# Two-layer gated cross-attention: order of the quads in layer 0, and later inputs loaded inside its loop

## Chip, cores and metric

The kernel runs on one core of a Trainium2 chip. The metric is the device time in microseconds of one execution. Engines are named as in the profile: PE (TensorE matmul), PEld (its weight loads), DVE (VectorE), ACT (ScalarE), POOL (GpSimd), SP (SyncE, which here only issues DMAs).

## The reference

```python
x = x + tanh(g_xattn[0]) * L0_xattn(layernorm(x), ctx, ...)   # 16 heads of 16, scores over 375 keys
x = x + tanh(g_ffn[0])   * L0_ffn(layernorm(x), ...)          # a gated recurrence over the 32 items
x = x + tanh(g_xattn[1]) * L1_xattn(layernorm(x), ctx, ...)   # 16 heads of 64
x = x + tanh(g_ffn[1])   * L1_ffn(layernorm(x), ...)          # 64 experts, 8 for each row, and a shared one
```

`x` is 32 items of 112 rows of 256, `ctx` 32 items of 375 rows of 128, all float32. The change concerns the first line alone: for each item, queries from the normalised `x`, keys and values from `ctx`, softmax over 375 keys for each of 16 heads, the weighted values, and an output projection.

## The kernel before, in words

The kernel has four stages, one after the other: layer 0's attention (in the profile from the start to about 702 us), its recurrence (to about 900 us), layer 1's attention with the routing, and the experts. Items come in eight groups of four (`G = 4`). The tiles `xs[g]` and `cts[g]` hold a group's `x` and its transposed context for the whole kernel.

Layer 0's attention works in *quads*: quad `n` is heads `4*(n%4)` to `4*(n%4)+3` of item `n // 4`, four heads of 16 channels, each on its own 32 partitions (rows 0 to 15 of the 32 hold the channels, row 16 a one in the keys and, in the second round, the negated maximum in the queries). One quad needs:

- the keys: `keys0(n)` makes the keys of two quads, `n` and `n + 1`, with one product `pk` (L414); ACT adds the bias (`k`, L419), and eight DMAs on SP's queue copy 16 rows each into `kT` (L421). There are six `kT` tiles.
- the queries of a whole group: `queries0` (product `pq` L396, DVE `q` L401, sixteen DMAs `qp` on SP's queue, L405). They need the group's statistics (`rstd0`: DVE L142 and L143, then POOL `rs` L371 and L372) and the turned normalised rows (`turned0`: DVE `xn` L379, PE L386).
- the scores twice. `quad(n, js, m, ks)` makes scores `sc` of quad `n` for two heads (L447), of which DVE takes the negated maximum `nm` (L451); and, for quad `m = n - 2`, whose maxima are known, transposed scores `st` with the maximum already subtracted (L462), of which ACT takes the exponential `pT` (L468). `with_max(n)` turns the maxima (`pm`, L474) and adds them to the queries (`qa`, DVE L478).
- `values0(b, kc)`: a third of an item's values (`pv`, L432; ACT copy L436), and `values_of(n)`: the weighted values `pav` (L491), copied by DVE (`oU`, L495).
- for each item, once: `divided` (`pn`, L502), `turned_back` (`pb`, L514), `output_rows` (`po`, L179), with DVE's `to_a` L183, `x` L172 and new statistics.

The order on PE, DVE and ACT is written out by hand (`manual_schedule`): each of these engines runs its instructions in the order of the program. SP and POOL are ordered by the tile framework. `sc` and `st` share a ring of five PSUM buffers (`ps_s`), everything else on PE a ring of three (`ps_m`). One iteration `n` of the loop (L530) is, before the change:

```python
quad(n, (0, 1), n - 2, (2, 3))
values_of(n - 3); keys0(n + 2) if n is even; values0(b, g) if g < 3; with_max(n - 1)
quad(n, (2, 3), n - 2, (0, 1))
# then, by n: rstd0 / turned0 / queries0 of the next group, divided / turned_back / output_rows
```

Before the loop, SP loads the first group's `x` and `ctx`, and POOL issues the loads of the other seven groups (L327, L330). Behind these fourteen loads in POOL's queue stand its memsets of `qp`, `v` and `nm` (L344 to L357), the first group's `rs` (L371, L372), and the halving of a weight of a later stage (`sdn`, L664).

Of the kernel before, what the change touches and what calls it, by code (L numbers as in the profile page):

```python
# [39 lines left out]
B, S, D = 32, 112, 256  # L40
# [3 lines left out]
G = 4  # L44
NG = B // G
# [20 lines left out]
def flamingo_kernel(ctx: ExitStack, tc: tile.TileContext, a: dict, out: bass.AP):  # L66
    nc = tc.nc
# [59 lines left out]
    xs = [const.tile([S, G, D], F32, tag=f"x{g}", name=f"x{g}") for g in range(NG)]  # L127
# [181 lines left out]
    with ExitStack() as att:  # L309
        cpool = att.enter_context(tc.tile_pool(name="ctxT", bufs=1))  # L310
        cts = [cpool.tile([DC, G, LKV], F32, tag=f"c{g}", name=f"c{g}") for g in range(NG)]


        with ExitStack() as ph:
# [8 lines left out]
            nc.sync.dma_start(cts[0], a["ctxT"][:, 0:G, :])  # L323
            nc.sync.dma_start(wv, a["wv0"])
            nc.sync.dma_start(wo, a["wo0"].rearrange("(c p) m -> p c m", p=128))
            for g in range(1, NG):
                nc.gpsimd.dma_start(  # L327
                    xs[g], a["x"][g * G : (g + 1) * G].rearrange("b s d -> s b d")
                )
                nc.gpsimd.dma_start(cts[g], a["ctxT"][:, g * G : (g + 1) * G, :])  # L330


            one = wp.tile([128, 1], F32, tag="one", name="one0")
# [28 lines left out]
            ps_s = ph.enter_context(tc.tile_pool(name="ps_s0", bufs=5, space=PSUM))  # L362
            ps_m = ph.enter_context(tc.tile_pool(name="ps_m0", bufs=3, space=PSUM))
            xTs, qas, pTs, outs = {}, {}, {}, {}

            def rstd0(g):
                t0 = g * G
                for b in range(t0, t0 + G):
                    row_stats(b)
                rs = small.tile([S, G], F32, tag="rs", name=f"rs0_{g}")  # L370
                nc.gpsimd.tensor_scalar(rs, stats[:, t0 : t0 + G, 1], EPS, None, ALU.add)  # L371
                nc.gpsimd.tensor_tensor(rs, rs, half, ALU.pow)  # L372
                return rs

            def turned0(g, rs):
                xT = xTs[g] = kvp.tile([128, 2, GT], F32, tag="xT", name=f"xTa_{g}", bufs=1)
                xn = work.tile([S, G, D], F32, tag="xn", name=f"xn_a0_{g}")
                for j in range(G):
                    nc.vector.tensor_scalar(  # L379
                        xn[:, j, :], xs[g][:, j, :], stats[:, g * G + j, 0:1], rs[:, j : j + 1],  # L380
                        ALU.subtract, ALU.mult,
                    )
                for c in range(2):
                    pt = ps_m.tile([128, GT], F32, tag="mm", name=f"ptx_a0_{g}_{c}")
                    for j in range(G):
                        nc.tensor.transpose(  # L386
                            pt[:, j * S : (j + 1) * S], xn[:, j, c * 128 : (c + 1) * 128],
                            ident[:S, :S],
                        )
                    nc.vector.tensor_copy(xT[:, c, :], pt)  # L390
# [19 lines left out]
            def keys0(n):  # L410

                b, i = n // 4, n % 4 // 2
                pk = ps_m.tile([128, LKV], F32, tag="mm", name=f"pk0_{n}")
                nc.tensor.matmul(  # L414
                    pk, wk[:, 128 * i : 128 * i + 128], cts[b // G][:, b % G, :],
                    start=True, stop=True,
                )
                k = kvp.tile([128, LKV], F32, tag="k", name=f"k0_{n}")
                nc.scalar.activation(k, pk, AF.Identity, bias=cols[:, C_BK + i : C_BK + i + 1])  # L419
                for h in range(8):  # L420
                    nc.sync.dma_start(  # L421
                        kTs[(n + h // 4) % 6][h % 4 * 32 : h % 4 * 32 + 16, :],
                        k[16 * h : 16 * h + 16, :],
                    )
# [4 lines left out]
            def values0(b, kc):  # L429
                pv = ps_m.tile([KC, 2, NH // 2, 16], F32, tag="mm", name=f"pv0_{b}_{kc}")  # L430
                for r in range(2):
                    nc.tensor.matmul(  # L432
                        pv[:, r], cts[b // G][:, b % G, kc * KC : (kc + 1) * KC],
                        wv_of[:, r, r], start=True, stop=True,
                    )
                nc.scalar.copy(  # L436
                    vs[b % 2][:, kc, :, :16].rearrange("p (a r) j -> p r a j", r=2), pv
                )

            def quad(n, js, m, ks):  # L440


                if 0 <= n < 4 * B:
                    b, g, j0 = n // 4, n % 4, n // 4 % G * S
                    for j in js:
                        sc = ps_s.tile([S, LKV], F32, tag="s", name=f"sc0_{n}_{j}")
                        nc.tensor.matmul(  # L447
                            sc, qps[b // G % 2][32 * j : 32 * j + 32, g, j0 : j0 + S],
                            kTs[n % 6][32 * j : 32 * j + 32, :], start=True, stop=True,
                        )  # L450
                        nc.vector.tensor_reduce(  # L451
                            nms[n % 3][:, j, 16:17], sc, AX.X, ALU.max, negate=True
                        )
                if 0 <= m < 4 * B:
                    if m not in pTs:
                        pTs[m] = pp.tile([KC, 4, NKC, S], F32, tag="pT", name=f"pT0_{m}")
                    st = {
                        j: ps_s.tile([KC, NKC, S], F32, tag="s", name=f"st0_{m}_{j}") for j in ks
                    }
                    for kc in range(NKC):  # L460
                        for j in ks:
                            nc.tensor.matmul(  # L462
                                st[j][:, kc, :],
                                kTs[m % 6][32 * j : 32 * j + 32, kc * KC : (kc + 1) * KC],
                                qas[m][32 * j : 32 * j + 32, :], start=True, stop=True,
                            )
                    for j in ks:
                        nc.scalar.activation(pTs[m][:, j], st[j], AF.Exp)  # L468

            def with_max(n):  # L470

                b, g, j0 = n // 4, n % 4, n // 4 % G * S
                pm = ps_m.tile([128, S], F32, tag="mm", name=f"pm0_{n}")
                nc.tensor.transpose(  # L474
                    pm, nms[n % 3].rearrange("p h j -> p (h j)"), ident[:S, :S]
                )
                qa = qas[n] = kvp.tile([128, S], F32, tag="qa", name=f"qa_{n}", bufs=3)
                nc.vector.tensor_tensor(  # L478
                    qa, pm, qps[b // G % 2][:, g, j0 : j0 + S], ALU.add
                )  # L480

            def values_of(n):
                b, g = n // 4, n % 4
                pT, v = pTs.pop(n), vs[b % 2]
                del qas[n]
                if g == 0:
                    outs[b] = kvp.tile([128, 4, S], F32, tag="oU", name=f"oU_{b}")
                po = ps_m.tile([128, S], F32, tag="mm", name=f"pav0_{n}")
                for kc in range(NKC):
                    for j in range(4):  # L490
                        nc.tensor.matmul(  # L491
                            po[32 * j : 32 * j + 32, :], v[:, kc, 4 * g + j, :], pT[:, j, kc, :],
                            start=(kc == 0), stop=(kc == NKC - 1),
                        )
                nc.vector.tensor_copy(outs[b][:, g, :], po)  # L495
# [33 lines left out]
            rs = None  # L529
            for n in range(4 * B + 6):  # L530
                b, g = n // 4, n % 4
                quad(n, (0, 1), n - 2, (2, 3))
                if 0 <= n - 3 < 4 * B:
                    values_of(n - 3)
                if n % 2 == 0 and n + 2 < 4 * B:
                    keys0(n + 2)
                if b < B and g < NKC:
                    values0(b, g)
                if 0 <= n - 1 < 4 * B:
                    with_max(n - 1)  # L540
                quad(n, (2, 3), n - 2, (0, 1))
                if b // G + 1 < NG and b % G == 1 and g == 3:
                    rs = rstd0(b // G + 1)
                if b // G + 1 < NG and b % G == 2 and g == 1:
                    turned0(b // G + 1, rs)
                if b // G + 1 < NG and b % G == 2 and g >= 2:
                    queries0(b // G + 1, g - 2)
                if g == 3 and b >= 1:
                    divided(b - 1)
                elif g == 0 and b >= 2:  # L550
                    turned_back(b - 2)
                elif g == 1 and b >= 2:
                    output_rows(pools, "a0", b - 2, outs.pop(b - 2), wo, 2, R_BO0, 0)
# [510 lines left out]
    for b in range(B):  # L1064
# [9 lines left out]
        if b % G == G - 1:  # L1074
            g = b // G
# [58 lines left out]
```

## Time and profile before

| | us |
|---|---|
| three runs | 2758.73, 2759.26, 2775.71 |
| median | 2759.26 |
| the profiled execution | 2965.47, span 2963.8 |
| PE busy in it | 2466.7 (83%) |
| DVE, ACT, POOL busy | 1787.5, 1158.1, 589.3 |

A profile gives each instruction with its engine, source line, start and duration, and what ended the idle time before it. `x2` behind a line counts the instructions merged into it. In the chain of waits a line is start, length and what ran; in the timeline it is start, length, engine, line, operation, tiles and shapes, and in square brackets the engine's idle time before it and its releaser. In the table of stretches the columns are the stretch and its length, the busy time of PE, PEld, DVE, ACT and POOL with counts, the clock granted to PE as a share of full speed, the DMA engines' busy share, and GB/s. `SPq` is a DMA being issued on SP's queue.

### The profile page before, as it was taken

To read this page: it belongs to the slowest core of one execution; us is meant where nothing else is said; L and a number is where in the kernel's file an instruction comes from. 1 tells how busy PE (TensorE), PEld (TensorE's weight loads), DVE (VectorE), ACT (ScalarE), POOL (GpSimd) and SP (SyncE) were. 2 spreads that over 40 slices of the span, in tenths; PEclk is the share of its full clock that TensorE was granted. 3 is DMA by queue.
4 is the path that set the end of the run, shared out by engine and by line. 5 is a ranking of instruction groups with operands and counts; after the bars stand their busy time and mean duration, and the time that the engine had idled before them with its cause. 6 is when DMAs were issued, how large, how long until landed. Compare 5 with 4: busy or idle time off the path is not lost.

```text
span 2963.8 us, 57837 instructions
## 1 busy us (share of the span) xinstructions
PE 2466.7 (83%) x20884; PEld 1900.2 (64%) x20884; DVE 1787.5 (60%) x4995; ACT 1158.1 (39%) x3019; POOL 589.3 (20%) x671
## 2 busy tenths in 40 slices
PE   4999999999997999897979999897976478888820
PEld 2666676777995776675757666575754366776720
DVE  2666666665327667575666767566665445555557
ACT  1433444443333554443535444443533133333310
POOL 3000000000000001204031211304032465555520
PEclk9999999999999999998989999998988699999965
DMA  5111100114001000101010000101011955555469
GB/s 170 28 26 26 26 24 24 27 29 159 2 1 43 1 1 20 36 1 55 1 43 13 30 27 11 45 1 55 1 37 54 306 172 151 148 146 151 130 183 271
DMA packets 121528, 198.21 MB, mean 67 GB/s; under 512 B 27399, under 2 KB 97113, under 8 KB 117664
## 3 DMA queue, kind: packets, MB, share of 16 engines
q1 hardware_dynamic: 78624, 102.50, 12.6%
q0 software_dynamic: 30176, 79.57, 8.2%
q10 hardware_dynamic: 12448, 12.45, 1.3%
q8 instruction: 171, 2.80, 0.4%
q14 instruction: 109, 0.89, 0.1%
HBM read 104.11 MB, written 82.71 MB: 63 GB/s over the span
## 4 chain that ended last, share of the span: by engine, by line
PE 66%; DVE 12%; issue 7%; DMA 5%; POOL 3%; SPq 3%; another core or an unknown queue 2%; ACT 1%; POOLq 0%; DVEq 0%; ACTq 0%
PE pv L710 6%; PE sc L447 5%; PE pk L695 5%; PE pt_a L761 5%; PE ps_a L732 5%; PE pav L782 4%; PE st L462 4%; PE pq L682 4%; PE po_a L797 3%; PE pg L590 3%; PE pav L491 3%; PE pg L611 3%; DMA y<-yrows 2%; PE py L1021 2%
## 5 line engine op out<-in xcount | busy, mean ns | idle before, releaser
L737 ACT ACTIVATE p_a<-ps_a,nmax_a 112x375 f32<-112x375 f32 x512 | 286.8, 572 | 430.8 <-DVE nmax_a L736 407.5
L1032 POOL DMA_INDIRECT yrows<-yblk,dst x288 | 280.9, 975 | 221.2 <-ACT yblk L1025 80.7
L468 ACT ACTIVATE pT<-st 125x336 f32<-125x336 f32 x512 | 202.7, 448 | 310.4 <-PE st L462 310.4
L710 PE MATMUL pv<-wv,c 128*125 128x256 f32 x768 | 227.1, 407 | 107.5 <-DVE oT L787 104.8
L451 DVE TENSOR_REDUCE nm<-sc 112x1 f32<-112x375 f32 x512 | 256.3, 541 | 90.5 <-PE st L462 64.2
L761 PEld LDWEIGHTS pt_a<-ident,p_a 112*125 112x125 f32 x1536 | 236.5, 196 | 104.3 <-issue 22.7
L301 POOL DMA_INDIRECT xrows<-row,at x256 | 247.9, 968 | 248.3 <-DVE at L299 171.6
L447 PE MATMUL sc<-kT,qp 32*112 32x375 f32 x1024 | 268.3, 532 | 17.7 <-DMA kT<-k 14.0
L736 DVE TENSOR_REDUCE nmax_a<-ps_a 112x1 f32<-112x375 f32 x512 | 245.2, 540 | 35.3 <-PE ps_a L732 26.9
L761 PE MATMUL pt_a<-ident,p_a 112*125 112x112 f32 x1536 | 240.2, 279 | 18.7 <-issue 16.0
L462 PE MATMUL st<-qa,kT 32*125 32x112 f32 x3072 | 238.5, 287 | 0.0
L695 PE MATMUL pk<-c,wk 128*128 128x375 f32 x512 | 218.1, 509 | 3.9 <-issue 3.6
L710 PEld LDWEIGHTS pv<-wv,c 128*125 128x125 f32 x768 | 130.9, 197 | 127.6 <-DVE oT L787 114.4
L462 PEld LDWEIGHTS st<-qa,kT 32*125 32x125 f32 x3072 | 192.3, 187 | 15.9 <-DVE nm L451 15.2
L732 PE MATMUL ps_a<-kT,qT 64*112 64x375 f32 x1024 | 198.6, 507 | 0.0
L782 PEld LDWEIGHTS pav<-pT_a,v 125*64 125x64 f32 x3072 | 148.0, 137 | 69.7 <-issue 51.4
L749 DVE TENSOR_SCALAR p_a<-p_a,inv_a 112x375 f32<-112x375 f32 x512 | 178.8, 412 | 4.6
L699 ACT COPY kT<-pk 128x375 f32<-128x375 f32 x256 | 121.3, 474 | 149.3 <-PE pk L695 80.0
L782 PE MATMUL pav<-pT_a,v 125*64 125x112 f32 x3072 | 176.5, 263 | 0.3 <-issue 0.2
L996 PE MATMUL ph<-wall,xbT 128*128 x896 | 147.1, 294 | 20.1 <-issue 13.2
L195 POOL TENSOR_SCALAR rs<-stats 112x4 f32<-112x4 f32 (+1 forms) x9 | 2.0, 226 | 735.3 <-DVE stats L143 735.2
L797 PE MATMUL po_a<-wo,oT 128*112 128x256 f32 x512 | 144.3, 402 | 3.4 <-issue 3.3
(227 smaller groups left out, 4390.8 us busy)
## 6 DMA issues: line engine op xcount, KB each, us to landing
xblk<-xrows SPq DMA_DIRECT2D x288, 140.0 KB
y<-yrows SPq DMA_DIRECT2D x32, 896.0 KB
kT<-k SPq DMA_DIRECT2D x512, 23.4 KB
xrows<-blank POOLq DMA_DIRECT2D x1, 8960.0 KB
wall<-in_w_up SPq DMA_DIRECT2D x8, 1024.0 KB
wall<-in_w_down ACTq DMA_DIRECT2D x8, 1024.0 KB
c<-in_ctxT POOLq DMA_DIRECT2D x7, 750.0 KB
yrows<-yblk,dst POOLq DMA_INDIRECT x288
```

The lines of the kernel that those rows point to most:

```text
L301: disjoint("xrows", nc.gpsimd.indirect_dma_start(out=xrows[:, :], out_offset=bass.IndirectOffsetOnAxis(ap=at[:, j, k : k + 1], axis=0), in ...
L447: nc.tensor.matmul(sc, qps[b // G % 2][32 * j : 32 * j + 32, g, j0 : j0 + S], kTs[n % 6][32 * j : 32 * j + 32, :], start=True, stop=True,)
L451: nc.vector.tensor_reduce(nms[n % 3][:, j, 16:17], sc, AX.X, ALU.max, negate=True)
L462: nc.tensor.matmul(st[j][:, kc, :], kTs[m % 6][32 * j : 32 * j + 32, kc * KC : (kc + 1) * KC], qas[m][32 * j : 32 * j + 32, :], start=True ...
L695: nc.tensor.matmul(pk, wk[:, c * 128 : (c + 1) * 128], cts[b // G][:, b % G, :], start=True, stop=True,)
L710: nc.tensor.matmul(pv[:, i, :], ct[:, (lo + i) * KC : (lo + i + 1) * KC], wv[:, g * 256 : (g + 1) * 256], start=True, stop=True,)
L732: nc.tensor.matmul(sc, qT[r0 : r0 + 64, 2 * g + i, j0 : j0 + S], kT[r0 : r0 + 64, i, :], start=True, stop=True,)
L736: nc.vector.tensor_reduce(nmax[:, j : j + 1], sc, AX.X, ALU.max, negate=True)
L737: nc.scalar.activation(p[:, j, :], sc, AF.Exp, bias=nmax[:, j : j + 1], accum_out=tot[:, j : j + 1],)
L761: nc.tensor.transpose(pt[:, j * S : (j + 1) * S], p[:, j, kc * KC : (kc + 1) * KC], ident[:S, :S],)
L782: nc.tensor.matmul(po[64 * r : 64 * r + 64, i, :], v[:, kc, 64 * j : 64 * j + 64], pT[:, kc, j * S : (j + 1) * S], start=(kc == 0), stop=( ...
L1032: disjoint("yrows", nc.gpsimd.indirect_dma_start(out=yrows[:, :], out_offset=bass.IndirectOffsetOnAxis(ap=dst32[:, 2 * n + i : 2 * n + i + ...
```

## The change

The loads of groups 1 to 7 leave POOL's queue. They are issued on ACT's queue inside the loop, a pair at the first quad of each group for the group that follows. Inside an iteration, `values_of` and `with_max` stand between the two calls of `quad`, and `keys0` and `values0` stand behind the second. Line numbers grow by up to 3.

```diff
-            for g in range(1, NG):
-                nc.gpsimd.dma_start(
-                    xs[g], a["x"][g * G : (g + 1) * G].rearrange("b s d -> s b d")
-                )
-                nc.gpsimd.dma_start(cts[g], a["ctxT"][:, g * G : (g + 1) * G, :])
...
+            def inputs(g):
+                nc.scalar.dma_start(
+                    xs[g], a["x"][g * G : (g + 1) * G].rearrange("b s d -> s b d")
+                )
+                nc.scalar.dma_start(cts[g], a["ctxT"][:, g * G : (g + 1) * G, :])
...
                 b, g = n // 4, n % 4
+                if b // G + 1 < NG and b % G == 0 and g == 0:
+                    inputs(b // G + 1)
                 quad(n, (0, 1), n - 2, (2, 3))
                 if 0 <= n - 3 < 4 * B:
                     values_of(n - 3)
+                if 0 <= n - 1 < 4 * B:
+                    with_max(n - 1)
+                quad(n, (2, 3), n - 2, (0, 1))
                 if n % 2 == 0 and n + 2 < 4 * B:
                     keys0(n + 2)
                 if b < B and g < NKC:
                     values0(b, g)
-                if 0 <= n - 1 < 4 * B:
-                    with_max(n - 1)
-                quad(n, (2, 3), n - 2, (0, 1))
```

## The prediction

> **What bounds the kernel now.** I read the chain of waits first, over the opening 60 us. It shows what the start hangs on.
>
> ```profile
> 7.32 17.75 DMA c<-in_ctxT
> 25.08 0.28 issue
> 25.36 0.55 POOL c L330
> 25.91 3.13 POOL qp L344 x2
> 29.04 2.64 POOL v L350 x2
> ...
> 32.71 0.86 POOL sdn L664
> 33.57 1.03 POOL rs L372
> 34.62 0.43 DVE xn_a L379
> ```
>
> POOL issues fourteen loads; the later ones wait for earlier ones to land. Behind them in its queue stand its memsets and the inverse deviation `rs`, and the first normalised rows wait for `rs`. The statistics were ready at 11.01 (last L143, timeline), so the core idles until 34.62.
>
> Second, the timeline of one ordinary item, for what a quad costs. An iteration has two halves (`quad`): two score products (sc, L447) beside six transposed ones (st, L462). F is the first, S the second.
>
> ```profile
> 316.27 0.57 PE L447 MATMUL sc<-kT,qp 32*112 32x375 f32 x2
> ...
> 317.12 0.41 PE L514 MATMUL pb<-ident,on 112*128 112x112 f32 x2
> 317.18 1.00 DVE L451 TENSOR_REDUCE nm<-sc 112x1 f32<-112x375 f32 x2 [0.53 <-PE st L462]
> 317.34 0.79 ACT L468 ACTIVATE pT<-st 125x336 f32<-125x336 f32 x2 [0.66 <-PE st L462]
> 317.46 0.59 PEld L447 LDWEIGHTS sc<-kT,qp 32*112 32x112 f32 x4
> ...
> 318.24 0.73 PEld L462 LDWEIGHTS st<-qa,kT 32*125 32x125 f32 x12 [0.19 <-DVE nm L451]
> ...
> 319.08 0.54 PEld L491 LDWEIGHTS pav<-pT,v 125*32 125x32 f32 x24
> ```
>
> S starts at 316.27 and lasts 0.85 (pb follows at 317.12). DVE reads its maxima until 318.18, and only then, 1.97 after S began, does st of the next F find a free buffer (`ps_s` has five; st2 takes that of sc3). F so lasts 1.62 in place of 0.85. A half needs 1.97 - 0.85 = 1.12 us of other PE work behind it, or PE waits. PE looks 83% busy on the page because its ends are modelled; this wait is inside.
>
> Third, the timeline once per group of four items, where the queries are copied.
>
> ```profile
> 264.39 4.94 SPq L421 DMA_DIRECT2D kT<-k  x8
> ...
> 269.43 12.18 SPq L405 DMA_DIRECT2D qp<-q  x16
> ...
> 281.71 8.20 SPq L421 DMA_DIRECT2D kT<-k  x9
> ...
> 283.63 1.64 PE L447 MATMUL sc<-kT,qp 32*112 32x375 f32 x2 [2.76 <-DMA kT<-k]
> ```
>
> SP issues 24 copies back to back; the next keys, ready at 274.8, leave at 281.71, and PE waits 2.76. The stretch table then shows the granted clock halved.
>
> ```profile
> 283.50:287.00 3.50, 3.37 (x40) 2.77 (x40) 1.10 (x2) 0.79 (x2) 0.00 (x0) 0.50 0.16 41
> ```
>
> [...] Here waits of 1.48 to 2.76 were followed by a 0.5 clock in four of seven groups, waits of 1.08 to 1.53 not in three: it depends on the phase.
>
> **The change, part by part.**
>
> *Loads off POOL.* Removed: 21.8 us between POOL's `sdn` load (ends 4.07) and its memsets (25.91). The memsets, 6.4 us, then end at 10.5; the statistics end at 11.0; rs 0.25, sdn 0.86 and rs 1.03 with small gaps give 13.3. xn starts there and not at 34.62: -21.3. The first group's inputs and weights remain, about 2.8 MB, at the 285 GB/s of the first 40 us some 10 us: in place before 15. If x0 lands sooner without the other 8 MB, up to 1.2 more.
>
> *Loads on ACT.* Fourteen issues of about 0.45 (the two weight loads on ACT took 0.40 and 0.45), 6.3 us in all, in ACT's 310 us of waiting for st (waits view): nothing on the path; without that cover 6.3. In the built order every DMA waits for the last one on its completion semaphore, eight in rotation: a load waits for key copies an iteration old (landed), with the exponentials queued behind it on ACT; the seventh and eighth key copies, and in the first group one query copy, wait on SP for a load. A pair is 1.2 MB, 4.2 us at 285 GB/s. In the loop those rows are needed an iteration later: nothing, at most 1 us a group. In the first group the query copy may lose up to 1 us; I take 0.5. Start: -20.8, bounds -17 (all 4.2 us exposed) and -22.5.
>
> *The order inside an iteration.* No instruction is added. From the timeline, PE work in the gaps: pav 0.71, pk 0.73, pv 0.55, pm 0.25, pb 0.34, pn 0.57, po 1.05. Before, F to S held pav, pk, pv, pm (enough), S to F only pb, po, nothing or pn, for quads 0 to 3. Waits by the 1.12 rule: 0.78, 0.07, 1.12, 0.55; the trace has 0.77, 0.06, 1.11, 0.53. Sum 2.5 of an item's 17.91.
> After, F to S holds pav and pm, 0.96: 0.16 short. S to F holds pk and pv (1.28), pv and po (1.60), or for quad 3 pn alone: 0.39 (0.55 less the 0.16 S lost). Quad 2 pays more: behind po DVE runs to_a, x and two statistics, so its maxima of F end 2.7 us after F begins (304.51 to 307.13, and 0.06); S is reached after 1.81: 0.87. Quad 0's S finds its buffers free. Sum 0.16 + 0.87 + 0.16 + 0.39 = 1.6. Gain 0.9 an item.
>
> *Once per group.* Quads 0 to 7 gain 1.65, 14 and 15 0.9. Around quad 8 DVE's four statistics (2.2 us, 246.52 to 248.73) make S wait 1.8 in place of 2.0 spread before; at quad 9 pv hides 0.53 of PE's 1.46 wait for xn: together 0.4. Against: quad 10's k now comes after S (S waits for DVE as above, half ends F + 3.5), pk and two exponentials: its copies leave at F + 5.1, before at F + 3.1 to 3.9. SP then needs the same 19.2 (264.39 to 283.63) to quad 14, so this stretch loses 1.2 to 2.0, say 1.6, whatever PE saves in it; PE waits about 4 us there, and the halved clock, which cost 2 to 3.5 us in four of seven groups, comes nearly always: -1.3; the shorter xn wait returns 0.4. Net +0.45; seven groups 3.2. Outside them: quads 110 on, 4.5 items, 4.0; quads 3 to 9 of the start 1.2. Total -8.4, bounds +8 (clock lost in other places too) and -25 (no clock loss, SP's copies faster without a profile).
>
> *Key copies elsewhere.* k leaves SP about 1.3 later in its iteration. A copy lands 1.8 to 1.9 after issue (chain of waits); by my timing the second row lands at F + 6.9 for a use at F + 8.5: nothing.
>
> Sum: -20.8 - 8.4 = -29.2 of the profiled execution's 2965.47 us (span 2963.8). The runs' median is 2759.26, 206 less; where the profile adds these the trace doesn't say, so I carry the microseconds over unscaled: 2730.
>
> **Rivals.** (A) SP's queue decides more than one stretch: order gains nothing and loses about 1.2 us a group, 8 in all: 2759 - 21 + 8 = 2746. For: SP's 24 copies; against: SP idles outside that stretch. (B) The order pays fully: DVE's tails fit better than my hand timing, half of 2.5 us for 28 items and no clock loss: 35 us with the start 56: 2703. For: PE waits in three of four gaps; against: DVE's chain of 1.97 per half stays. (C) Slower: key rows late. Each of some 55 key products outside the queue stretch now has 1.6 us of slack; if landing takes over 3.5 us (now 1.9), every second quad waits. At 0.4 us each the start's gain is gone; at 1.05 it is 58: 2759 - 21 + 58 = 2796. [...] DMA engines are 10% busy. (D) The loads stay early or x0 and c0 become the wait: the built order has the loads among the activations, and 10 us of transfer end before 15; at worst 10 back: 2740, inside the forecast's range.
>
> **How the numbers follow.** Forecast 0.68, with D, own range 2715 to 2743; A 0.13; B 0.13; C 0.06. About 1% (27.6 us) can be told from no change. The forecast's middle lies just past it, so 0.42 of its 0.68 is faster, with B 0.55; its other 0.26 and A make 0.39 within; C 0.06 slower. The range takes in A and part of B: 2712 to 2749.
>
> **What would show it.** Right: xn near 13 us; first S waits of 0.16 and no wait in quads 1 and 3's F; 0.9 quad 2 S waits; the key wait per group grown to about 4 us, then a 0.5 clock. Wrong: key waits on ordinary even quads, xn later than 17, an ordinary item above 17.9 us.

## The result, and the profile after

The changed kernel takes 2750.94 us (median of 20 runs, 2746.51 to 2764.03) where the kernel before takes 2761.38 (20 runs, 2754.49 to 2777.43): a ratio of 0.9959, 95% interval 0.9944 to 0.9974, which is 10.4 us. In a later set of runs the same pair gave 2972.07 and 2981.45 us (e7 below): 0.9958, 0.9935 to 0.9980. The prediction said 29.2, and its range of 2712 to 2749 us ends just below the measured time. One run each of e7, e11, e14 and e16 below counts as slow (over 1.5% above the fastest of its kernel); without it no median moves by more than 0.9 us.

The chain of waits of the changed kernel has no pieces in the first 60 us, so the timeline stands in for it. Columns: start, length, engine, line, operation, tiles, and in brackets the idle time before and what ended it.

```profile
3.48 0.60 POOL L135 DMA_DIRECT2D sdn<-in_ws_down  x1
4.07 3.14 POOL L339 MEMSET qp<- 128x1792 f32 x2
...
11.33 0.59 POOL L372 TENSOR_SCALAR rs<-stats 112x4 f32<-112x4 f32 x1 [0.89 <-DVE stats L143]
...
12.01 2.16 POOL L667 TENSOR_SCALAR sdn<-sdn 128x256 f32<-128x256 f32 x1
12.05 1.40 DVE L335 COPY kT<-one 128x375 f32<-128x375 f32 x5
14.14 1.05 POOL L373 TENSOR_TENSOR rs<-rs,half 112x4 f32<-112x4 f32 x1
15.22 1.39 DVE L380 TENSOR_SCALAR xn_a<-x,stats,rs 112x256 f32<-112x256 f32 x4 [1.77 <-POOL rs L373]
...
19.18 0.35 ACTq L362 DMA_DIRECT2D x<-in_x  x1
...
28.30 2.12 PE L448 MATMUL sc<-kT,qp 32*112 32x375 f32 x5 [5.39 <-DMA qp<-q]
```

POOL goes straight from its loads to its memsets; the 21.8 us of loads are gone. The first normalised rows start at 15.22 and not at 34.62, the first score product at 28.30 and not at 46.26.

The timeline of an ordinary item, quads 1 and 2 of it:

```profile
297.61 0.57 PE L448 MATMUL sc<-kT,qp 32*112 32x375 f32 x2
297.62 0.58 PE L463 MATMUL st<-qa,kT 32*125 32x112 f32 x6
...
299.42 0.57 PE L448 MATMUL sc<-kT,qp 32*112 32x375 f32 x2
299.58 0.47 PE L463 MATMUL st<-qa,kT 32*125 32x112 f32 x4
...
303.73 1.29 PE L448 MATMUL sc<-kT,qp 32*112 32x375 f32 x4
304.59 0.73 PEld L463 LDWEIGHTS st<-qa,kT 32*125 32x125 f32 x12 [0.19 <-DVE nm L452]
304.59 0.91 PE L463 MATMUL st<-qa,kT 32*125 32x112 f32 x12
305.43 0.90 PE L415 MATMUL pk<-c,wk 128*128 128x375 f32 x2
```

F of quad 1 (297.61) has st at once; S of quad 1 (299.42) has it 0.16 later; S of quad 2 (303.73) has it 0.86 later. The first pn of one item to the first pn of the next is 292.54 to 309.51, or 16.97; before it was 17.91.

The once-a-group stretch, the same group as was shown of the kernel before, and the granted clock behind it (columns of the stretch table as before; the clock is the column with 0.54):

```profile
246.79 5.26 SPq L422 DMA_DIRECT2D kT<-k  x8
252.16 10.87 SPq L406 DMA_DIRECT2D qp<-q  x16
263.13 11.98 SPq L422 DMA_DIRECT2D kT<-k  x13
265.09 1.15 PE L448 MATMUL sc<-kT,qp 32*112 32x375 f32 x3 [3.46 <-DMA kT<-k]
```

```profile
266.00:269.50 3.50, 3.50 (x53) 2.77 (x49) 1.62 (x4) 0.79 (x2) 0.00 (x0) 0.54 0.13 34
```

PE now waits 3.46 us for key rows where it waited 2.76. Over the seven groups these waits are 2.83, 3.30, 3.46, 3.61, 2.80, 2.74 and 4.13, or 3.27 in the mean; before the mean was 1.84.

One warning on the two profiles. They do not come from like conditions. Between the first query product of layer 1 and its last output product (the tile views, before first, then after) lie 1349 us before and 1246 after:

```profile
L682 PE MATMUL pq<-xTb,wq x512: 352/352/743, 938.8 to 2178.8; 128*128 128x224 f32 x171
L797 PE MATMUL po_a<-wo,oT x512: 376/379/470, 973.4 to 2287.6; 128*112 128x256 f32 x171
```

```profile
L685 PE MATMUL pq<-xTb,wq x512: 352/352/739, 914.2 to 2063.4; 128*128 128x224 f32 x171
L800 PE MATMUL po_a<-wo,oT x512: 379/379/470, 949.4 to 2160.5; 128*112 128x256 f32 x171
```

In the five later sets of runs, on chips 2, 10, 7, 8 and 8 by the record, the kernel before took 2963 to 2983 us; its profiled execution of 2965.47 is of that kind. The record names no chip for the runs of the result. The same changed kernel took 1365 us for this stretch in e7's profile (920.0 to 2285.4), so the 103 us are not the change's doing. I take the 206 us between profile and median for two chips, not for a cost of profiling; that it is the chip was not tested. They lie behind layer 0. In layer 0 the profiles of the changed kernel are nearer to each other: the last item's first `pn` stands at 674.01 in the profile after and at 680.75 in e7's. The kernel before, cut behind layer 0, took 713.0 us on chip 2 and 708.8 on chip 8; the changed one 696.2 and 697.9. I read differences of under 5 us between chips as undecided.

### The profile page after: what moved, and what is told of

Its sections match the earlier page's. It is cut to its first block, busy times and chain, and to the rows that moved or that the text cites. A ratio compares the mean times of both kernels' runs of the same rounds, so it can differ in the third digit from the quotient of the medians.

```text
span 2745.6 us, 57911 instructions
## 1 busy us (share of the span) xinstructions
PE 2411.1 (88%) x20884; PEld 1882.0 (69%) x20884; DVE 1776.0 (65%) x4995; ACT 1164.1 (42%) x3019; POOL 581.4 (21%) x657
## 5 line engine op out<-in xcount | busy, mean ns | idle before, releaser
L448 PE MATMUL sc<-kT,qp 32*112 32x375 f32 x1024 | 264.1, 542 | 33.3 <-DMA kT<-k 24.2
L713 PE MATMUL pv<-wv,c 128*125 128x256 f32 x768 | 217.9, 393 | 49.1 <-DVE oT L790 47.4
L771 DVE COPY pT_a<-pt_a 125x448 f32<-125x448 f32 x128 | 78.8, 616 | 115.7 <-PE pt_a L764 115.6
L448 PEld LDWEIGHTS sc<-kT,qp 32*112 32x112 f32 x1024 | 87.2, 178 | 90.6 <-issue 45.5
```

The costliest lines, as they stand in the source:

```text
L448: nc.tensor.matmul(sc, qps[b // G % 2][32 * j : 32 * j + 32, g, j0 : j0 + S], kTs[n % 6][32 * j : 32 * j + 32, :], start=True, stop=True,)
L713: nc.tensor.matmul(pv[:, i, :], ct[:, (lo + i) * KC : (lo + i + 1) * KC], wv[:, g * 256 : (g + 1) * 256], start=True, stop=True,)
```

## The experiments

I began with two theories. The first: layer 0 gains what the two profiles show (the stage behind it starts at 684.4 and not at 710.7, 26 us sooner), and a later stage gives back 15. The second: layer 0 itself gains only about 10 when it is timed. Where a later paragraph compares runs of different sets, the chips are 2 for e1 to e4, 10 for e5 to e8, 7 for e9 to e12 and 8 for e13 to e18.

**The parts alone.** e1_loads is the change without its last hunk (the order in the loop stays). e2_order is that hunk alone.

```diff
 # e1_loads, against the kernel before
-            for g in range(1, NG):
-                nc.gpsimd.dma_start(
...
+                if b // G + 1 < NG and b % G == 0 and g == 0:
+                    inputs(b // G + 1)
 # e2_order, against the kernel before
+                if 0 <= n - 1 < 4 * B:
+                    with_max(n - 1)
+                quad(n, (2, 3), n - 2, (0, 1))
                 if n % 2 == 0 and n + 2 < 4 * B:
                     keys0(n + 2)
                 if b < B and g < NKC:
                     values0(b, g)
-                if 0 <= n - 1 < 4 * B:
-                    with_max(n - 1)
-                quad(n, (2, 3), n - 2, (0, 1))
```

> Only the loads move from POOL's queue to ACT's inside the loop; the order of the iteration stays as before. Theory 1 (both parts work in layer 0 and a later stage gives some 15 us back): layer 0 ends about 19 us earlier in the profile (xn at 15.2 in place of 34.6), and the time falls by 19 less what the later stages give back, 2742 to 2757. Theory 2 (without a profile the start is worth less, or the order costs): the profile shows the same 19, the time falls by the whole 19 if the order is at fault (2742), by 10 or less if the start is.

Measured: 2944.09 us against 2968.73, ratio 0.9918 (0.9889 to 0.9946), 24.6 us.

> Only the order of the iteration changes; POOL keeps the loads ahead of its memsets. Both theories: xn stays near 34.6 us; in the profile an ordinary item takes 16.98 us in place of 17.91 and layer 0 ends about 7 us earlier. Theory 1: the time falls by 7 less what later stages give back, so 2754 to 2769. Theory 2 with the order at fault: the time rises by 5 to 10 us, 2766 to 2771.

Measured: 2962.41 us, ratio 0.9968 (0.9947 to 0.9989), some 6 to 10 us. The parts alone give 31 us and both together 10, so either they hinder each other or the whole kernel is too coarse a scale: its single runs spread over 28 to 37 us.

**Layer 0 alone.** Everything behind layer 0 is left out, and the output is x as it stands there.

```diff
-        with ExitStack() as ph:
-            wp = ph.enter_context(tc.tile_pool(name="wr", bufs=1))
...
+    for g in range(NG):
+        nc.scalar.dma_start(out[g * G : (g + 1) * G].rearrange("b s d -> s b d"), xs[g])
```

> The kernel before with everything behind layer 0's attention left out: the output is x after the first line of the reference. Its time is that of the first 702 us of the profile and the writing of the output, about 712 us. It is the base for the same cut of the changed kernel.

> The changed kernel with everything behind layer 0's attention left out. Theory 1: 26 us below the same cut of the kernel before, as in the profiles (first product of the recurrence at 684.4 in place of 710.7). Theory 2: only about 10 below, the whole change seen in the full kernel.

Measured: 713.0 us (710.75 to 717.29) and 696.22 (695.86 to 697.16): 16.8 us. Runs now spread over 1 to 7 us.

**Where behind it?** e7_after_again is the changed kernel unedited; e5_cut1_before and e6_cut1_after leave out only the experts' blocks and their sum (the same cut, one stage later).

> The whole change again, beside the kernel before on the same chip as the other three of this set. Theory 1 (layer 0 gives 17 to 26 us and a later stage hands some of it back): about 10 us faster than the kernel before, ratio 0.996. Theory 2 (the loads alone and the order alone add up, and the first measurement met a chip on which the parts are worth less): about 25 to 30 us faster, ratio 0.990, where the parts alone gave 24 and 6 to 9 us.

> The kernel before, cut behind layer 1: the blocks of the experts and their sum are left out, and the output is x as it stands there. The comparison is with e6_cut1_after. Expected about 2270 to 2300 us on a chip where the whole kernel takes 2969; about 2080 on one where it takes 2761.

> The changed kernel with the same part left out. Theory 1 with the loss in layer 1's attention (its start meets other traffic, and its stage is bound by something that does not start earlier): the difference to e5_cut1_before is about 10 us. Theory 1 with the loss among the experts: it is 17 to 26 us, and only the whole kernel shows 10. Theory 2: 25 to 30 us here as well.

Measured: 2972.07 against 2981.45; 2353.23 (2334.26 to 2362.94) against 2340.07 (2326.0 to 2347.29). So 16.8 us by layer 0 (10.9 in the second pair below), 13.2 by the end of layer 1, 9 to 10 in the whole. The ranges of e5 and e6 overlap: no later stage is shown to give anything back, so nothing is left to carry the first theory. The gain is small already in layer 0.

**Free the queue.** e8_after_qpool issues the sixteen query copies of a group on POOL's queue.

```diff
                 for h in range(8):
-                    nc.sync.dma_start(
+                    nc.gpsimd.dma_start(
                         qps[g % 2][h % 4 * 32 : h % 4 * 32 + 16, 2 * i + h // 4, :],
```

> The changed kernel with one edit: the sixteen copies of a group's queries are issued by GpSimd's queue and no longer by SyncE's, so that the key rows which come behind them in SyncE's queue start some 8 to 9 us sooner. If the wait for key rows once a group (2.7 to 4.1 us of TensorE each, seven times in the trace of the changed kernel, with a slower clock behind it) is what eats the order's gain, this is 10 to 20 us faster than e7_after_again and the waits fall under 0.5 us each. If that wait is only where another wait would stand, it is within 5 us of e7_after_again. If GpSimd's queue is slow to issue, the queries of a group come late and it is slower by up to 15 us.

Measured: 2941.19 us (2924.51 to 2958.09), ratio to the kernel before 0.9854 (0.9805 to 0.9903), 31 us less than e7: more than was expected. It beats both kernels. The queue of copies matters; I made that theory Q.

**The four combinations, layer 0 alone.** e9_cut0_loads and e10_cut0_order are e1 and e2 with the cut; e11_cut0_qpool is e8 with the cut; e12_cut0_before_qpool is the kernel before with e8's edit and the cut.

> The change's loads alone (old order in the iteration), with everything behind layer 0 left out, to be read against the kernel before (713.0 us) and the changed kernel (696.2 us) with the same part left out. Theory Q (SyncE's queue of query and key copies sets the length of a group of four items, so that the order gains nothing and the start is all of the gain): 692 to 698 us. The prediction's sum (the order pays 8 of 29 us): about 704 us, since the order's 8 us would be missing. Theory X (loads and order hinder each other, as the whole kernels' 24, 6 and 10 us suggest): 690 us or less.

> The change's order alone (loads still on GpSimd's queue), the same part left out. Theory Q: 711 to 716 us, as the kernel before. The prediction's sum: 705 us. Theory X: 705 us or less, and with the loads' gain the two add up to clearly more than the 16.8 us that both together gave.

> The changed kernel with the queries' sixteen copies on GpSimd's queue, the same part left out. Theory Q: seven groups without the wait for key rows (2.9 to 4.5 us each) and without the slower clock behind it (1.7 us for each window of 3.4 us): 696 less 7 x 5 = about 661 us, mean clock 0.97 instead of 0.94. If the whole kernel's gain from this edit came from elsewhere: above 680 us.

> The kernel before with the same one edit, the same part left out. It has waits for key rows of 1.4 to 2.7 us in each group, 13.5 us in seven. Theory Q in its narrow form (the queue costs only where PE waits for key rows): 713 less 13.5 less up to 6 for the clock = about 695 us; the new order's worth with the queue free is then what is left between this and e11_cut0_qpool after the start's 20 us, about 14 us or 2 us a group. If the queue's cost in the old order is hidden by other waits: 705 to 713 us.

Measured: 690.67 (685.82 to 694.78), 709.9 (704.16 to 712.9), 656.3 (650.2 to 662.73) and 682.27 us (680.62 to 683.66). The loads alone bring 18 to 22 us. The order alone brings nothing that two chips can tell apart, and beside the moved loads it costs 5.5 (7.2 against e14 below), little more than chips differ by; that it does not pay is plain. The stretch behind the key wait shows one reason (stretches of 4 us, loads alone first, then the whole change; the clock is third from the end):

```profile
266.00:270.00 4.00, 4.00 (x63) 2.94 (x62) 1.86 (x6) 1.63 (x4) 0.00 (x0) 1.00 0.14 34
270.00:274.00 4.00, 4.00 (x66) 2.73 (x61) 2.50 (x6) 1.58 (x4) 0.00 (x0) 1.00 0.16 38
274.00:278.00 4.00, 4.00 (x56) 2.95 (x54) 2.77 (x7) 2.03 (x5) 0.00 (x0) 1.00 0.69 188
```

```profile
266.00:270.00 4.00, 3.66 (x41) 2.85 (x41) 1.16 (x3) 0.79 (x2) 0.00 (x0) 0.56 0.14 36
270.00:274.00 4.00, 4.00 (x29) 2.92 (x32) 1.49 (x4) 1.41 (x4) 0.00 (x0) 0.59 0.02 6
274.00:278.00 4.00, 4.00 (x63) 2.73 (x59) 2.86 (x8) 1.80 (x5) 0.00 (x0) 1.00 0.25 29
278.00:282.00 4.00, 3.21 (x52) 2.25 (x53) 2.19 (x6) 0.79 (x2) 0.00 (x0) 1.00 0.94 264
```

Behind a key wait of 1.15 us the clock stayed at 1.00 in e9; behind one of 3.76 it was 0.56 and 0.59 in the next two stretches in e4. In stretches of 1 us the clock is halved in blocks of 3.4 us or multiples. From 67 us on, e9 has five such blocks, e4 seventeen, and each a piece at its end (mean granted clock of the two profiled runs 0.971 and 0.938). At a share of 0.50 a block costs at most 1.7 us of full-clock time by my estimate: up to 20 us for the twelve more. (The profile of e9 is of its fastest run, 685.82 us, so the two profiles lie 10 us apart where the medians lie 5.5.)

**Two leftovers of that set.** In the last row above the DMA engines are 94% busy with the next group's loads, and small key waits stand beside them (0.42 at 278.44 in e4). e13_cut0_after_later issues the loads four quads later; e14_cut0_after_again and e15_cut0_before_again are e4 and e3 on its chip. e16_cut0_loads_qpool is e9 with the query copies on POOL.

```diff
 # e13_cut0_after_later, against e4
-                if b // G + 1 < NG and b % G == 0 and g == 0:
+                if b // G + 1 < NG and b % G == 1 and g == 0:
```

> The changed kernel with each group's loads issued four quads later (at the second item of a group and no longer at its first), everything behind layer 0 left out. If the loads' transfers, which follow closely on the wait for key rows, hold up the key copies behind it (theory L): the small extra waits for key rows behind that wait go, the third item of a group comes down from 17.9 us towards 17.0, and the time is 5 to 8 us below e14_cut0_after_again. If the difference between the order alone and the order beside the loads was one of chips or of the clock's phase: within 2 us of e14_cut0_after_again.

> The changed kernel with the same part left out, again, as the reference on this chip. 696 us if chips don't matter for layer 0.

> The kernel before with the same part left out, again. 713 us if chips don't matter for layer 0; its distance to e14_cut0_after_again is 16.8 us if the first pair is right.

> The loads moved, the order as before, and the queries' copies on GpSimd's queue, the same part left out: against e11_cut0_qpool (656.3 us, the same with the new order) it gives what the new order is worth with SyncE's queue free. If the prediction's timing of the halves is right (0.9 us an ordinary item, 28 items, less the wait at the third quad and what the clock takes): 14 to 25 us slower than e11_cut0_qpool, 670 to 681 us. If the order is worth little anyway: 656 to 664 us.

Measured: 693.46 (693.17 to 696.4), 697.88 (691.6 to 702.14), 708.78 (705.33 to 712.41) and 667.23 us (665.12 to 675.37). Moving the loads brings 4.4 us, less than expected and with overlapping runs, and the small waits moved with them: the pair issued at 296.20 has a key wait of 0.74 at 302.75. With SP's queue free the new order is worth 667.23 - 656.3 = 11 us, where 14 to 25 was expected. Theory Q explains that the order did not pay, and not how much it could.

**Which of the moved calls?** Two calls go behind S, `keys0` and `values0`; `with_max` stands right ahead of S in both orders. Of the two, only `keys0` feeds SP's queue. e17_cut0_keys_early is e4 with `keys0` alone put back ahead of S, so that against e9 it moves `values0` alone; e18_cut0_keys_early_qpool is the same edit to e11.

```diff
                     values_of(n - 3)
+                if n % 2 == 0 and n + 2 < 4 * B:
+                    keys0(n + 2)
                 if 0 <= n - 1 < 4 * B:
                     with_max(n - 1)
                 quad(n, (2, 3), n - 2, (0, 1))
-                if n % 2 == 0 and n + 2 < 4 * B:
-                    keys0(n + 2)
```

> The changed kernel with keys0 alone put back ahead of the second half of the quad (values0 stays behind it), everything behind layer 0 left out. If the later keys are what eats the order's gain: the wait for key rows once a group falls from 3 to 4.5 us to 1 to 2 us as in the old order, and the time is below the loads alone (690.7 us), about 683 to 688 us. If the order loses by its halves and not by the keys: 696 us or more.

> The same, with the queries' copies on GpSimd's queue; to be read against e11_cut0_qpool (656.3 us). If the later keys still cost there (the waits of 0.3 to 1.2 us during the loads' transfers): 650 to 655 us. If the filling behind the second half matters more (keys0's product no longer stands there at even quads, which then lack some 0.2 to 0.8 us of other work): 657 to 664 us.

Measured: 657.04 us (655.73 to 659.79) and 626.85 (626.24 to 628.58), both far below what any theory expected; e4 took 696.22 on chip 2 and e14, the same kernel, 697.88 on chip 8. The waits view of e4, then of e17, then of e18 (engine, line, what it waited for: us in total, times, longest):

```profile
PE sc L448 <- DMA kT<-k: 26.3, 11, 4.5
```

```profile
PE sc L448 <- DMA kT<-k: 15.9, 7, 3.2
PE sc L448 <- DMA qp<-q: 5.2, 1, 5.2
```

```profile
PE sc L448 <- DMA qp<-q: 4.9, 1, 4.9
```

The key waits are only 10 us of the 39 between e4 and e17; the small ones are gone altogether. Another part is in the timelines. Quad 8, the one with DVE's four statistics, first in e4, then in e17:

```profile
229.80 0.57 PE L448 MATMUL sc<-kT,qp 32*112 32x375 f32 x2
...
231.99 0.88 PE L448 MATMUL sc<-kT,qp 32*112 32x375 f32 x2
233.38 0.88 PE L448 MATMUL sc<-kT,qp 32*112 32x375 f32 x2 [0.51 <-DVE nm L452]
233.83 0.91 PE L463 MATMUL st<-qa,kT 32*125 32x112 f32 x12
...
236.13 0.57 PE L448 MATMUL sc<-kT,qp 32*112 32x375 f32 x2
```

```profile
220.69 0.97 PE L448 MATMUL sc<-kT,qp 32*112 32x375 f32 x4
...
222.78 0.90 PE L415 MATMUL pk<-c,wk 128*128 128x375 f32 x2
...
224.27 1.02 PE L448 MATMUL sc<-kT,qp 32*112 32x375 f32 x4
...
226.54 0.57 PE L448 MATMUL sc<-kT,qp 32*112 32x375 f32 x2
```

And quad 2 of an ordinary item in e17 (in the changed kernel it is the one that starts at 301.92 above):

```profile
292.24 0.57 PE L448 MATMUL sc<-kT,qp 32*112 32x375 f32 x2
...
293.80 0.90 PE L415 MATMUL pk<-c,wk 128*128 128x375 f32 x2
...
294.73 0.57 PE L448 MATMUL sc<-kT,qp 32*112 32x375 f32 x2
...
296.38 0.57 PE L448 MATMUL sc<-kT,qp 32*112 32x375 f32 x2
```

In both, DVE's maxima are late between F and S, and there pk fills PE's time. F to the next F is 5.85 us in quad 8 (in e4 229.80 to 236.13, 6.33) and 4.14 in quad 2 (301.92 to 306.70 above, 4.78). Behind S, where the change puts it, pk comes when that time is already lost. The old order had pk there as well, and needed 5.80 and 3.86. Not all of it is a net gain: quads 0, 1 and 3 are slower in e17 than in e4, and an ordinary item is shorter by 0.14 (16.98 to 16.84).

In the changed kernel's own trace the wait at quad 8 is also a second place where the clock halves, right behind it:

```profile
230.00:232.00 2.00, 1.49 (x15) 1.00 (x14) 2.00 (x7) 0.00 (x0) 1.06 (x2) 1.00 0.06 16
232.00:234.00 2.00, 2.00 (x9) 1.32 (x7) 0.49 (x2) 1.07 (x3) 0.00 (x0) 0.54 0.00 0
234.00:236.00 2.00, 2.00 (x21) 1.65 (x20) 0.39 (x1) 0.68 (x2) 0.00 (x0) 0.60 0.05 12
```

Group by group, from the first pn of one item to the next, in the mean of seven groups. The last three rows are the same items where no halved clock and no wait for key rows falls into them; item 2 is taken there from the runs with the query copies on POOL (e16, e11, e18).

| us | item 1 | item 2 (key wait) | item 3 | item 4 | group |
|---|---|---|---|---|---|
| e9, old order | 24.5 | 20.3 | 17.9 | 17.9 | 80.6 |
| e4, the change | 24.9 | 22.9 | 17.6 | 17.2 | 82.5 |
| e17, keys0 left ahead of S | 23.1 | 20.6 | 16.8 | 16.8 | 77.4 |
| old order, undisturbed | 24.3 | 17.3 | 17.9 | 17.9 | 77.4 |
| the change, undisturbed | 24.2 | 16.7 | 17.0 | 17.0 | 74.8 |
| keys0 ahead of S, undisturbed | 23.1 | 16.3 | 16.8 | 16.8 | 73.0 |

Undisturbed, the change's order is worth 2.6 us a group. But waits for keys and the halved clock take 7.6 of a group in e4 and 3.2 in e9, which is 4.5 more. From e4 to e17 the filling gives 1.9 a group, 13 us in seven; the 3.2 less of waits and clock give 23, of which 10 are the key waits. Together that is 36 us, as between the two profiles; the medians have 39.

Even without the queue's stretch the change leaves something: e11 to e18 is 29 us with hardly a wait for keys in either (4.1 us and none). e18 has the halved clock only at its start and its end, where e11 has seven blocks between, and each of its groups takes 73.0 us. Neither e17 nor e18 was run as a whole kernel, and `keys0` alone behind S, with `values0` in its old place, was not run.

## Why the prediction was wrong

The step that failed is "Once per group": what the later keys lose there was priced too low. In total the order was to gain 8.4 us, and beside the moved loads it cost 5.5 (690.67 to 696.22; 7.2 against e14). The prediction had a group lose 1.6 us by the key wait and 1.3 by the clock, with 0.4 back for a shorter xn wait: 2.5. From e9 to e4 the waits and the clock took 4.5 more of each group, against the 2.6 that the order gains in it. The start held.

- **The start: right.** Predicted 20.8 us; the loads alone gave 18 to 22 in layer 0 and 24.6 in the whole kernel. Inside it, xn came at 15.2 and not at 13.3: `sdn` took 2.16 us and not 0.86, beside DVE's five kT copies, and `rs` 0.59 and not 0.25. The first scores came 18.0 sooner, the first pn 20.4 (83.49 to 63.08). Single profiles scatter here: in e1's the first pn stands at 70.65, with the clock halved for 23.9 of the first 67 us, against 13.7 before and 17.1 after.
- **The ordinary item: right to the hundredths.** 0.16 at S, 0.86 at S of quad 2, nothing at F of quads 1 and 3; 0.94 an item predicted as 0.9. But a group has only two ordinary items, and in e4 they returned 1.1 a group (35.8 to 34.7) and not 1.8: blocks of halved clock and small key waits reach into them.
- **The key wait: right in place and size.** The keys of quad 10 left at F + 5.0 in e4 (predicted 5.1); the wait grew by 1.43 in the profiles of before and after, and by 1.96 from e9 to e4 (predicted 1.6).
- **The clock: too cheap.** It was priced at 1.3 us a group. From e9 to e4 there are twelve more blocks of 3.4 us in seven groups, up to 2.9 us a group. In the whole kernels it is less (e1 to e7: from ten to seventeen, up to 1.7). Single executions differ. The prediction put a halved clock behind the key wait alone. It also comes behind the wait at quad 8, which the prediction saw (1.8 us) and gave no clock. The kernel before has it in that item too, behind the 1.46 us wait for xn at quad 9 (blocks of 3.41 us at 177.0, 258.9, 426.1 and 590.0): the prediction used that wait and missed its clock. With pk ahead of S and the xn wait at 0.68, e17 and e18 have no such block.
- **Quads 8 and 9: a gain that the item does not keep.** 0.4 was predicted. Undisturbed they gain 0.72 (13.62 to 12.90 from F of 8 to F of 10), but quad 10 gives 0.63 back (5.65 to 6.28), since its maxima are late as those of quad 2 are, and item 1 of a group went from 24.5 to 24.9 with the clock.
- **Quads 14 and 15: a slip.** The 0.9 does not follow from the prediction's own waits for quads 2 and 3 of an item, 1.67 before and 1.42 after; undisturbed the two gain 0.14 (8.31 to 8.17).
- **"Key copies elsewhere: nothing" was wrong by little.** The loads' transfers show: small waits of 0.2 to 0.8 us behind them. e13 puts what they cost at 4.4 us, within the scatter of its runs.
- **What was not asked at all** is what each of the moved calls is worth alone. `values0` behind S gives, with `keys0` left in place, 690.67 - 657.04 = 33.6 us by the medians (26 between the two profiles); `keys0` behind S as well takes 39 back. The prediction's sum treated the two as one.

So the time of rival A is what came: start full, order minus 8, 13 us in all against the 10.4 measured, for the reason it names (SP's queue) and two that it does not (the clock, and pk taken from the place where it filled). That its number is so near is partly luck. Rival B's 35 us is near what the order pays without `keys0`. C did not come: no steady wait on even quads. D neither: the opening transfers are over before the loads of the second group start at 19.18.

The 206 us carried over unscaled were the right choice for a wrong worry: they lay behind layer 0, and layer 0 takes the same to a few microseconds.

Open: how the 39 us of `keys0` divide exactly. By the undisturbed items some 13 are the filling and by the waits view 10 the key waits; the clock (seven blocks in e17 where e4 has seventeen, at most 17 us) has what is left. The three act on each other, and no run holds two of them still. That `sdn` took longer beside DVE's copies was seen, and its cause was not tried.

## What to carry to other kernels

When an edit moves several calls, price and try each alone: here it was the one whose result leaves through a queue that was already late, with little work on its own engine (`keys0`: 39 us by the medians). Put filler where the partner engine is late, not where the count of instructions looks thin. And take the period of the whole repeating group as the unit: an ordinary item that is 0.94 us shorter says nothing while another item of the group grows by 2.6.

## What the runs showed of the hardware

- The clock was halved in blocks of 3.41 us or multiples (before: 0.50 from 200.85 to 204.26 and from 282.77 to 289.60). All 41 of them in the profile before start whole multiples of 3.41 us apart, and so do all 32 in the one after (before: 176.96, 200.85, 258.88 and 282.77 are 7, 17 and 7 blocks apart). They also followed waits of PE far shorter than a block, and no length of wait decided alone. A key wait of 3.76 us (e4) was followed by two blocks, one of 1.48 (before, 199.93) by one and one of 1.16 (e11, 270.41) by two, but one of 1.53 (before, 119.05) and one of 1.15 (e9) by none. At quad 8, st came 1.85 us after S began in the changed kernel (229.42 to 231.27) and a block followed; in e4 it came after 1.84 and none did. Seven waits for xn in the profile before were of 1.46 or 1.47 us: the four that ended 1.5 to 2.0 us ahead of one of these multiples (174.94, 257.36, 424.10, 587.96) were followed by a block there, the three that ended 2.2 to 3.1 us ahead of one (95.32, 341.97, 508.62) by none. That is the phase of the prediction.
- A load that had to wait held POOL's queue: before, it stood idle for 2.49 us ahead of the load of `x` at 10.35, until `su` had landed, which it had issued eight loads earlier.
- Sixteen small copies took SP 10.0 to 12.2 us to issue (before, eight groups) and POOL two times 4.16 us (e11, 242.96 and 247.47), so a queue of copies is priced like an engine.
- While ACT's loads of 1.2 MB ran at up to 264 GB/s (e4, 278 to 282), small copies issued by SP came late (waits of 0.2 to 0.8 us in e4), and the waits moved with the loads in e13 (0.74 at 302.75).
- The median of the kernel before was 2761 us in one set of runs and 2963 to 2983 in five others; that the chip is the cause was not tested. Cut behind layer 0, the same kernels differed by 4.2 and 1.7 us between chips 2 and 8.
